# A quantized feed-forward stage whose instructions are put in a fixed order, five turns deep

## The chip, the cores and the metric

The kernel runs on one core of a Trainium2 chip. A core has five engines that follow their own instruction streams and meet at semaphores: TensorE (matmuls and transposes, written PE in profiles, its weight loads PEld), VectorE (DVE), ScalarE (ACT), GpSimd (POOL) and SyncE (SP, which issues the DMAs here). The metric is the device time of one execution in microseconds (us). Before the change the median of 8 runs is 2927.6 us, the lowest 2920.58 and the highest 2935.03.

## The reference, cut to what matters

The program computes a two-layer network on 64 x 64 tokens of 256 values. Layer 0 is attention and a feed-forward, layer 1 a recurrence with a state-space block and a mixture of experts. The change touches only the feed-forward of layer 0, `x = x + ffn(cond2(x, cond))`:

```python
ys = y * scale
d = rsqrt(einsum('bi,io->bo', ys * ys, weight * weight) + EPS)
out = einsum('bsi,io->bso', Efou * ys[:, None, :], weight) * d[:, None, :]
# bitlinear, twice: 256 -> 1024, then 1024 -> 256
x_norm = x * rsqrt(mean(square(x)) + EPS_NORM) * w
scale = 127.0 / clip(max(abs(x_norm)), 1e-5, None)
x_q = clip(round(x_norm * scale), -128, 127) / scale
h = x_q @ weight_quant(w1).T
h = act_scale * square(relu(h)) + act_bias      # between the two
```

Every token is thus multiplied by its sample's row `ys` and by a weight, scaled by `d`, normalised, rounded to whole numbers, multiplied by a ternary weight, squared behind a relu, normalised and rounded again, multiplied by a second ternary weight and added to x.

## The kernel before, in words

The residual x lies transposed in on-chip memory (`g.xT`: 128 partitions x 2 x 4096 tokens). `ffn0` (L560) walks over 16 pairs of token tiles; a pair is 2 x 128 tokens, `TP` = 256. The work on one pair `p` is cut into seven stages:

- `product` (L614): GpSimd multiplies the pair's x by `ys` into `xs` (L617). TensorE multiplies `xs` by `Wc` (L628) and spreads the rows of `d` with a selecting matmul (L632). ScalarE copies that spread out of PSUM (`dt`, L634), VectorE multiplies both into `gm` (L635), and ScalarE takes the sums of squares of `gm` (L581, which for a tile of 1024 columns is the "large" form).
- `quantize_in` (L638, through `quantized`, L584): first a refined inverse root of the mean of squares, on two numbers per partition. GpSimd forms the mean (L592), ScalarE takes the root (L593), VectorE the reciprocal (L594), and GpSimd a Newton step in five small operations (L595 to L599). Then VectorE multiplies the tile by the norm's weight (L600), takes the largest absolute value (L601), forms the scale (L603, L604), scales and rounds (L609), and writes whole numbers as bf16 (L611). GpSimd forms the scale back (L605, L606).
- `turn`: four transposes of that into PSUM (L645), copied by ScalarE to `qT` (L647).
- `up`: 2 x 2 matmul groups to 1024 columns (L655), a relu with a scale (L656) and a square (L658) on ScalarE, `act_scale` and `act_bias` on VectorE (L659), and the large sums of squares on ScalarE (L581).
- `quantize`: `quantized` again, on `h` (128 x 2048).
- `turn_back`: sixteen transposes (L670), copied by ScalarE to `q2T` in two halves (L671).
- `down`: sixteen matmuls (L678), the scale back on ScalarE (`o`, L680), four transposes (L682), the residual add on VectorE into xT (L684) and a DMA of x to HBM on SP's queue.

The loop writes them for a skew of seven: in turn `t`, pair `t` is in `product`, pair `t-1` in `quantize_in`, and so on, the latest stage first. That is only the order in which the operations are written. The framework's scheduler then orders each engine's stream by a priority that follows the written order and by its own estimate of when things are ready, places tiles in the pools' buffers, and adds the semaphores. A tile pool with `bufs=2` gives a name two buffers; PSUM has four buffers of the tag `ps` and four of the tag `acc`. What stands next to what on an engine is thus the scheduler's choice.

Behind the stage comes the recurrence of layer 1 (`rnn`), 64 steps that each need the one before. Its first matmuls (L723) over the second half of the samples need the last pair's residual add.

Of the kernel before, what the change touches and what calls it, by code (L numbers as in the profile page):

```python
# [13 lines left out]
F32 = mybir.dt.float32  # L14
BF16 = mybir.dt.bfloat16
I32 = mybir.dt.int32
AF = mybir.ActivationFunctionType
ALU = mybir.AluOpType
AX = mybir.AxisListType
PSUM = bass.MemoryType.PSUM  # L20

P = 128
B, L, D = 64, 64, 256
NT = B * L
CH = 512
NCH = NT // CH
KD = D // P
CB = CH // L
NTT = NT // P
EPS = 1e-8  # L30
MAGIC = 12582912.0
# [45 lines left out]
def bank(g, shape=(P, CH), dt=F32, tag="ps"):  # L77
    tag = g.tag or tag
    return g.psum.tile(list(shape), dt, tag=tag, name=tag)
# [477 lines left out]
    return chain(one, two, (squares, sums)), (lambda: rsqrt(nc, d2[:, 0, :], d, d2[:, 1, :]),)  # L557


def ffn0(g, w):  # L560


    nc, tc = g.nc, g.tc
    F = w.F
    NF = F // P
    T = 2
    TP = T * P
    NP = NT // TP
    BP = TP // L
    with (  # L570
        tc.tile_pool(name="f1", bufs=1) as p1,
        tc.tile_pool(name="f2", bufs=2) as p2,
        tc.tile_pool(name="f3", bufs=3) as p3,
    ):
        w1q, m1, w2q, m2, ys, d = w.w1q, w.m1, w.w2q, w.m2, w.ys, w.d

        def square_sums(x, n):
            ss = p2.tile([P, T], F32, name=f"ss{n}")
            for t in range(T):
                junk = p1.tile([P, n], BF16, name=f"junk{n}")  # L580
                nc.scalar.activation(junk, x[:, t, :], AF.Square, accum_out=ss[:, t : t + 1])  # L581
            return ss

        def quantized(x, ss, wn, mean, n):  # L584

            st = p3.tile([P, 7, T], F32, name=f"st{n}")  # L590
            v, rs, t, most, am, sc, back = (st[:, i, :] for i in range(7))
            nc.gpsimd.tensor_scalar(v, ss, 1.0 / n, EPS, ALU.mult, ALU.add)  # L592
            nc.scalar.activation(rs, v, AF.Sqrt)  # L593
            nc.vector.reciprocal(rs, rs)  # L594
            nc.gpsimd.tensor_mul(t, rs, rs)  # L595
            nc.gpsimd.tensor_mul(t, t, v)
            nc.gpsimd.tensor_scalar(t, t, -0.5, 1.5, ALU.mult, ALU.add)
            nc.gpsimd.tensor_mul(rs, rs, t)
            nc.gpsimd.tensor_scalar(most, rs, 127.0 / 1e-5, None, ALU.mult)  # L599
            nc.vector.tensor_tensor(x, x, wn.unsqueeze(1).to_broadcast([P, T, n]), ALU.mult)  # L600
            nc.vector.tensor_reduce(am, x, AX.X, ALU.max, apply_absolute_value=True)  # L601

            nc.vector.reciprocal(sc, am)  # L603
            nc.vector.scalar_tensor_tensor(sc, sc, 127.0, most, ALU.mult, ALU.min)  # L604
            nc.gpsimd.tensor_mul(back, am, rs)  # L605
            nc.gpsimd.tensor_scalar(back, back, 1e-5, mean, ALU.max, ALU.mult)  # L606
            q = p2.tile([P, T, n], BF16, name=f"q{n}")
            for i in range(T):
                nc.vector.tensor_scalar(x[:, i, :], x[:, i, :], sc[:, i : i + 1], MAGIC, ALU.mult, ALU.add)  # L609

            nc.vector.tensor_scalar(q, x, MAGIC, 127.0, ALU.subtract, ALU.min)  # L611
            return q, back

        def product(p, v):  # L614
            tok = ts(p, TP)
            xs = p2.tile([P, KD, BP, L], F32, name="xs")
            nc.gpsimd.tensor_tensor(  # L617
                xs,
                g.xT[:, :, tok].rearrange("p k (b l) -> p k b l", l=L),
                ys[:, :, ts(p, BP)].unsqueeze(3).to_broadcast([P, KD, BP, L]),  # L620
                ALU.mult,
            )
            xs2 = xs.rearrange("p k b l -> p k (b l)")
            gm = p2.tile([P, T, D], F32, name="gm")
            for t in range(T):
                ps = bank(g, (P, 2, D))
                for k in range(KD):
                    nc.tensor.matmul(ps[:, 0, :], xs2[:, k, ts(t, P)], w.Wc[:, k, :], start=(k == 0), stop=(k == KD - 1))  # L628

                for j in range(2):  # L630
                    b = p * BP + 2 * t + j
                    nc.tensor.matmul(ps[ts(j, L), 1, :], g.ident[:B, b : b + 1].to_broadcast([B, L]), d, start=True, stop=True)  # L632
                dt = p2.tile([P, D], F32, name="dt")
                nc.scalar.copy(dt, ps[:, 1, :])  # L634
                nc.vector.tensor_mul(gm[:, t, :], ps[:, 0, :], dt)  # L635
            v.gm, v.ss1 = gm, square_sums(gm, D)

        def quantize_in(p, v):  # L638
            v.q1, v.back1 = quantized(v.gm, v.ss1, w.n1, m1, D)

        def turn(p, v):
            pt = bank(g, (P, KD, TP), BF16)
            for t in range(T):
                for k in range(KD):
                    nc.tensor.transpose(pt[:, k, ts(t, P)], v.q1[:, t, ts(k, P)], g.identb)  # L645
            v.qT = p2.tile([P, KD, TP], BF16, name="qT")
            nc.scalar.copy(v.qT, pt)  # L647

        def up(p, v):
            v.h = p3.tile([P, T, F], F32, name="h")  # L650
            for t in range(T):
                for f in range(F // CH):
                    ps = bank(g)
                    for k in range(KD):
                        nc.tensor.matmul(ps, v.qT[:, k, ts(t, P)], w1q[:, k, ts(f, CH)], start=(k == 0), stop=(k == KD - 1))  # L655
                    nc.scalar.activation(v.h[:, t, ts(f, CH)], ps, AF.Relu, scale=v.back1[:, t : t + 1])  # L656
                h = v.h[:, t, :]
                nc.scalar.activation(h, h, AF.Square)  # L658
                nc.vector.tensor_scalar(h, h, w.act[:, 0:1], w.act[:, 1:2], ALU.mult, ALU.add)  # L659
            v.ss = square_sums(v.h, F)  # L660

        def quantize(p, v):
            v.q2, v.back2 = quantized(v.h, v.ss, w.n2, m2, F)

        def turn_back(p, v):
            v.q2T = p2.tile([P, T, NF, P], BF16, name="q2T")
            for t in range(T):
                pt = bank(g, (P, NF, P), BF16, tag="acc")
                for f in range(NF):
                    nc.tensor.transpose(pt[:, f, :], v.q2[:, t, ts(f, P)], g.identb)  # L670
                nc.scalar.copy(v.q2T[:, t], pt)  # L671

        def down(p, v):
            po = bank(g, (P, KD, TP), tag="acc")
            for t in range(T):
                ps = bank(g, tag="acc")
                for f in range(NF):
                    nc.tensor.matmul(ps[:, :D], v.q2T[:, t, f, :], w2q[:, f, :], start=(f == 0), stop=(f == NF - 1))  # L678
                o = p2.tile([P, D], F32, name="o")
                nc.scalar.activation(o, ps[:, :D], AF.Copy, scale=v.back2[:, t : t + 1])  # L680
                for k in range(KD):
                    nc.tensor.transpose(po[:, k, ts(t, P)], o[:, ts(k, P)], g.ident)  # L682
            x = g.xT[:, :, ts(p, TP)]
            nc.vector.tensor_add(x, x, po)  # L684
            nc.sync.dma_start(g.x[:, :, ts(p, TP)], x)

        stages = (product, quantize_in, turn, up, quantize, turn_back, down)
        pairs = [SimpleNamespace() for _ in range(NP)]
        for turn_ in range(NP + len(stages) - 1):
            for i in reversed(range(len(stages))):  # L690
                p = turn_ - i
                if 0 <= p < NP:
                    stages[i](p, pairs[p])

# [1272 lines left out]
def tile_adaln_attn_ffn_d2(ctx: ExitStack, tc: tile.TileContext, a: dict, out: bass.AP):  # L1969
# [29 lines left out]
    close_attn()  # L1999

    ffn0(g, w_ffn0)
    close_ffn0()

# [101 lines left out]
```

## Time and profile before

| what | value |
|---|---|
| median of 8 runs | 2927.6 us |
| profiled execution | 2927.91 us, of which span 2925.9 us |
| granted TensorE clock, whole span | 0.912 |
| the stage: first `xs` to the end of the last residual add | 383.4 to 637.6 us |
| busy in 383 to 638 us (255 us): PE, PEld, DVE | 185.05, 108.21, 201.78 us |
| the same: ACT, POOL | 187.30, 127.15 us |
| granted TensorE clock in that stretch | 0.83 |

The profile is of one execution. A row of the timeline gives the start, the length, the engine, the line, the operation, the tile written and the tiles read, the shape, how many are merged, and in brackets the idle time before it with what ended it. A row of the waits gives the one who waited, the one waited for, the total, how often, and the longest. Lengths on an engine overlap a little, since it begins the next step before the last is written; where a step's share of the engine is wanted, starts are compared with starts. The granted clock is the share of full speed at which TensorE was let run.

### The profile page before, as it was taken

To read this page: it belongs to the slowest core of one execution; us is meant where nothing else is said; L and a number is where in the kernel's file an instruction comes from. 1 tells how busy PE (TensorE), PEld (TensorE's weight loads), DVE (VectorE), ACT (ScalarE), POOL (GpSimd) and SP (SyncE) were. 2 spreads that over 40 slices of the span, in tenths; PEclk is the share of its full clock that TensorE was granted. 3 is DMA by queue.
4 is the path that set the end of the run, shared out by engine and by line. 5 is a ranking of instruction groups with operands and counts; after the bars stand their busy time and mean duration, and the time that the engine had idled before them with its cause. 6 is when DMAs were issued, how large, how long until landed. Compare 5 with 4: busy or idle time off the path is not lost.

```text
span 2925.9 us, 34770 instructions
## 1 busy us (share of the span) xinstructions
PE 2418.3 (83%) x12148; PEld 1707.8 (58%) x12148; DVE 1756.9 (60%) x2955; ACT 1412.6 (48%) x2406; POOL 1306.5 (45%) x1117
## 2 busy tenths in 40 slices
PE   4889977779566888888778888788885989999995
PEld 4533434458244555555455555466763768888885
DVE  0567658850399979798979888873352523232322
ACT  1566557764555666666565757443331212222220
POOL 0022345430368676768576868654536251111110
PEclk9979988798677989899889999899997999999997
DMA  9999600020122212121112121315685746655555
GB/s 235 369 358 337 212 25 19 19 66 1 44 73 77 71 59 76 64 74 66 58 62 98 62 90 69 112 35 179 199 279 193 275 172 245 221 184 204 204 186 178
DMA packets 183076, 406.06 MB, mean 139 GB/s; under 512 B 25312, under 2 KB 89056, under 8 KB 177520
## 3 DMA queue, kind: packets, MB, share of 16 engines
q1 hardware_dynamic: 169456, 366.80, 37.1%
q0 software_dynamic: 13440, 36.98, 3.3%
q8 instruction: 98, 1.61, 0.2%
q14 instruction: 82, 0.67, 0.1%
HBM read 280.76 MB, written 144.98 MB: 146 GB/s over the span
## 4 chain that ended last, share of the span: by engine, by line
PE 43%; DVE 19%; ACT 9%; issue 8%; POOL 5%; DMA 2%; another core or an unknown queue 1%; DVEq 0%; SPq 0%; ACTq 0%; POOLq 0%
DVE hb L1009 11%; PE ps L1603 11%; PE acc L1501 8%; DVE hb L1011 3%; PE yp L1025 2%; PE mq L1739 2%; PE mp L906 2%; PE ps L1570 2%; PE mq L1755 2%; POOL hb L970 2%; DVE xc L851 1%; PE ps L745 1%; PE ps L628 1%; PE acc L745 1%
## 5 line engine op out<-in xcount | busy, mean ns | idle before, releaser
L970 POOL TENSOR_TENSOR hb<-dx,Bn 128x1024 f32<-128x1024 f32 x256 | 600.9, 2357 | 259.2 <-PE yp L1025 253.5
L1009 DVE TENSOR_TENSOR_SCAN hb<-dA,hb 128x512 f32<-128x512 f32 x512 | 603.1, 1209 | 34.7 <-ACT dA L977 32.3
L977 ACT ACTIVATE dA<-delta,A 128x504 f32<-128x504 f32 x512 | 344.4, 683 | 306.3 <-DVE hb L1009 297.5
L1025 PEld LDWEIGHTS yp<-ident,hb 128*128 128x128 f32 x2048 | 267.0, 151 | 180.0 <-issue 141.9
L1011 DVE TENSOR_TENSOR hb<-hb,cb 128x1024 f32<-128x1024 f32 x256 | 312.2, 1220 | 79.3 <-PE cb L922 62.0
L1603 PE MATMUL ps<-gxT,w 128*128 128x256 f32 (+1 forms) x1600 | 323.7, 361 | 0.8 <-DVE gxT L1478 0.8
L1603 PEld LDWEIGHTS ps<-gxT,w 128*128 128x128 f32 x1600 | 276.5, 190 | 46.1 <-issue 12.5
L1025 PE MATMUL yp<-ident,hb 128*128 128x128 f32 x2048 | 301.4, 291 | 0.0
L1739 PE MATMUL mq<-x,moe_s 128*128 128x256 f32 x896 | 253.8, 416 | 50.8 <-ACT up L1746 27.0
L1277 POOL DMA_INDIRECT ffn_y<-gy,to x72 | 69.2, 961 | 446.6 <-ACT gy L1503 434.7
L1739 PEld LDWEIGHTS mq<-x,moe_s 128*128 128x128 f32 x896 | 171.2, 207 | 117.0 <-ACT up L1746 35.9
L1607 DVE TENSOR_TENSOR gh<-gs,ps 128x256 f32<-128x256 f32 (+1 forms) x200 | 78.7, 394 | 219.3 <-ACT gs L1606 217.3
L922 PE MATMUL cb<-parts,pick 80*128 80x512 bf16 x256 | 104.8, 409 | 111.2 <-DVE hb L1011 94.0
L1501 PE MATMUL acc<-w,gh 128*128 128x256 f32 (+1 forms) x864 | 191.6, 392 | 2.0 <-issue 2.0
L1503 ACT ACTIVATE gy<-acc,wt 128x256 f32<-128x256 f32 x152 | 67.1, 472 | 254.7 <-PE acc L1501 225.1
L1606 ACT ACTIVATE gs<-ps 128x256 f32<-128x256 f32 (+1 forms) x200 | 72.3, 362 | 241.0 <-PE ps L1603 224.9
L1501 PEld LDWEIGHTS acc<-w,gh 128*128 128x128 f32 (+1 forms) x864 | 148.3, 192 | 34.5 <-issue 16.7
L426 POOL TENSOR_TENSOR E<-E,z 128x1024 f32<-128x1024 f32 x32 | 61.6, 1924 | 202.8 <-DVE z L425 123.5
L1501 PE MATMUL acc<-w,rh 128*128 128x256 f32 x320 | 86.3, 411 | 50.6 <-ACT rh L1572 44.8
L1277 POOL DMA_INDIRECT moe_y<-gy,to x80 | 77.2, 965 | 112.0 <-ACT gy L1503 91.4
L444 PE MATMUL out<-oT,M 128*128 128x512 f32 x256 | 120.1, 614 | 1.5 <-ACT oT L437 1.5
L1755 PE MATMUL mq<-moe_s,sh 128*128 128x256 f32 x448 | 115.4, 396 | 6.2 <-ACT up L1746 6.2
(462 smaller groups left out, 4469.4 us busy)
## 6 DMA issues: line engine op xcount, KB each, us to landing
w<-ffn_w SPq DMA_DIRECT2D x40, 2176.0 KB
Bn<-B SPq DMA_DIRECT2D x128, 512.0 KB
moe_x<-fill SPq DMA_DIRECT2D x130, 260.0 KB
ffn_x<-fill SPq DMA_DIRECT2D x129, 260.0 KB
w<-moe_w SPq DMA_DIRECT2D x48, 512.0 KB
ffn_w<-in_ffn_W_dram SPq DMA_DIRECT2D x16, 640.0 KB
gx<-moe_x SPq DMA_DIRECT2D x32, 260.0 KB
gx<-ffn_x SPq DMA_DIRECT2D x32, 260.0 KB
```

Source lines behind the costliest of these rows:

```text
L444: nc.tensor.matmul(ps, M[:, o, ts(k, P)], v.o[:, o], start=(o == 0), stop=(o == H // 2 - 1))
L922: nc.tensor.matmul(t, pick[:, n : n + 1].to_broadcast([rows, P]), v.parts, start=True, stop=True)
L970: nc.gpsimd.tensor_mul(hb, vs[c].dx[p], Bn[:, n % NB, :].unsqueeze(1).to_broadcast([P, PI, CH]))
L977: nc.scalar.activation(decays[s][i][:, :, 1:], seq(vs[c].delta[p][:, i, :])[:, :, 1:], AF.Exp, scale=w.A[:, p * PI + i, n : n + 1],)
L1009: ins = nc.vector.tensor_tensor_scan(h, dA[i].rearrange("p b l -> p (b l)"), h, 0.0, ALU.mult, ALU.add)
L1011: ins = nc.vector.tensor_tensor(hb, hb, cb.unsqueeze(1).to_broadcast([P, PI, CH]), ALU.mult)
L1025: nc.tensor.matmul(yp[i][:, t, :], hb[:, i, ts(t, P)], g.ident, start=(n == 0 and t == 0), stop=(n == S - 1 and t == CH // P - 1), is_tran ...
L1277: i = self.g.nc.gpsimd.indirect_dma_start(out=self.y, out_offset=bass.IndirectOffsetOnAxis(ap=to, axis=0), in_=y, in_offset=None)
L1501: nc.tensor.matmul(po[s], h, w, start=(i == 0), stop=(i == n - 1))
L1603: nc.tensor.matmul(ps[:, j, :], v.w12[:, k, ts(j * (full + 1) + i, P)], v.xT[:, k, :], start=(k == 0), stop=(k == KD - 1))
L1739: nc.tensor.matmul(ps[:, i % 2, :], w[:, k, ts(i, P)], xu[:, k, :], start=(k == 0), stop=(k == KD - 1))
L1755: nc.tensor.matmul(ps[:, t, :], h[:, i, ts(t, P)], self.s2[:, i, :], start=(i == 0), stop=(i == NS - 1))
```

## The change

A small class, `InOrder`, wraps an engine: every operation that is asked through it gets a mark with the engine's name, and the scheduler keeps marked operations of one name in the order in which they were written. All operations of `ffn0` on TensorE, VectorE, ScalarE and GpSimd go through such wrappers, so their order on each engine is that of the text. Work of other stages is not marked.

The stages are cut into smaller pieces and written out once per turn in a fixed order, `turn_at(n)`. In turn `n`, pair `n` is in `product`, `n-1` is quantized and turned, `n-2` is in `up`, `n-3` is quantized on its 1024 columns and turned back, and `n-4` goes `down`; so the depth is five turns in place of seven. The first operation of a pair, GpSimd's product `xs`, becomes a piece of its own (`spread`) and is written one turn early: behind VectorE's large product and the refined root, ahead of the large maximum. The two halves of `up` are parted by `lie_down` and `product`. No operation, shape or buffer count changes. Since each operation is now issued from inside the wrapper, a profile shows nearly all of the stage under the wrapper's one line.

```diff
+class InOrder:
+    def __getattr__(self, op):
+        def ask(*args, **kwargs):
+            ins = getattr(self.engine, op)(*args, **kwargs)
+            self.tc.stamp_issue_order_token(ins.ins, self.name)
+            return ins
+        return ask
...
-        def quantized(x, ss, wn, mean, n):
+        def quantized(x, st, wn, mean, n, *between):
...
+            ve.tensor_tensor(x, x, wn.unsqueeze(1).to_broadcast([P, T, n]), ALU.mult)
+            for other in between:
+                other()
+            ve.tensor_reduce(am, x, AX.X, ALU.max, apply_absolute_value=True)
...
-        stages = (product, quantize_in, turn, up, quantize, turn_back, down)
-        for turn_ in range(NP + len(stages) - 1):
-            for i in reversed(range(len(stages))):
-                p = turn_ - i
-                if 0 <= p < NP:
-                    stages[i](p, pairs[p])
+            def quantize(p, v):
+                rest = (lambda: better(v.st2)), (lambda: at(spread, n + 1))
+                v.q2, v.back2 = quantized(v.h, v.st2, w.n2, m2, F, *rest)
+            def quantize_in(p, v):
+                better(v.st1)
+                v.q1, v.back1 = quantized(v.gm, v.st1, w.n1, m1, D)
...
+            at(quantize_in, n - 1)
+            at(down, n - 4)
+            at(root_big, n - 3)
+            if 0 <= n - 3 < NP:
+                at(quantize, n - 3)
+            else:
+                at(spread, n + 1)
+            at(up, n - 2, 0)
+            at(lie_down, n - 4)
+            at(product, n)
+            at(up, n - 2, 1)
+            at(turn, n - 1)
+            at(turned, n - 1)
+            at(modulated, n)
+            at(root_small, n)
+            at(turn_back, n - 3)
+            at(add, n - 4)
+            at(scaled, n - 2)
+            at(sums, n - 2)
+        at(spread, 0)
+        for n in range(NP + 4):
+            turn_at(n)
```

The pieces: `roots` is the mean (L592) and the root, `better` the reciprocal and the Newton step, `modulated` the copies of `dt`, the product `gm` and its sums of squares, `turned` the copy to `qT`, `scaled` the step of L659, `sums` the large sums of squares, `lie_down` the four transposes of `o`, `add` the residual add with its DMA.

## The prediction

> **What bounds the kernel now.** I read first the tile view of the residual xT, which dates the stage; then the busy time by stretch with the granted clock; then the waits inside the stage; then the timeline of each engine over two pairs, for durations.
>
> The tile view of xT, then the busy times (columns: stretch, its length, then PE, PEld, DVE, ACT, POOL, then the granted TensorE clock, DMA):
>
> ```profile
> L684 DVE TENSOR_TENSOR xT<-xT,acc x16: 672/684/689, 438.7 to 636.9; 128x512 f32<-128x512 f32 x16
> ```
>
> ```profile
> 470.00:588.00 118.00, 89.51 (x510) 52.11 (x509) 98.63 (x166) 89.58 (x184) 60.05 (x134) 0.80 0.06 19
> 498.05:515.12 17.07, 12.19 (x90) 7.26 (x88) 15.34 (x25) 15.93 (x33) 9.94 (x18) 1.00 0.09 31
> 515.12:528.77 13.65, 11.33 (x40) 6.26 (x41) 9.88 (x19) 7.09 (x16) 5.47 (x17) 0.50 0.01 2
> ```
>
> The stage runs from 383.4 (first product) to 637.6 (the last residual add, 636.92 + 0.69); the recurrence behind it needs that add. No engine is full in the middle: DVE 98.63 of 118. The two lower rows show one period of 30.7 us, two pairs: TensorE has its full clock for 17.07 us, then half for 13.65 us, and then the other engines starve (ACT 7.09 of 13.65). A pair costs about 15.2 us.
>
> ```profile
> PE acc L678 <- ACT q2T L671: 34.1, 15, 4.0
> ...
> DVE st L604 <- POOL st L599: 19.3, 8, 3.6
> ```
>
> So before is bound by waits between engines: TensorE for the evicted transposes q2T, VectorE for the small steps on GpSimd.
>
> ```profile
> 500.35 2.15 POOL L595 TENSOR_TENSOR st<-st 128x2 f32<-128x2 f32 x1 [2.02 <-DVE st L594]
> ```
>
> ```profile
> 621.11 2.31 POOL L592 TENSOR_SCALAR st<-ss 128x2 f32<-128x2 f32 x1 [2.19 <-ACT junk L581]
> ```
>
> These two-element steps last 0.19 us at other places. Here they started beside VectorE's large product L600 (500.18 and 621.08, 2.27 us) and ended with it. Beside the maximum L601 they take 0.19.
>
> ```profile
> 513.20 1.25 ACT L656 ACTIVATE h<-ps,st 128x512 f32<-128x512 f32 x2
> 514.47 1.06 ACT L658 ACTIVATE h<-h 128x1024 f32<-128x1024 f32 x1
> 515.43 0.40 ACT L581 ACTIVATE junk<-gm 128x256 bf16<-128x256 f32 x1
> ...
> 515.83 1.90 ACT L671 COPY q2T<-acc 128x1024 bf16<-128x1024 bf16 x2
> 517.63 0.21 ACT L593 ACTIVATE st<-st 128x2 f32<-128x2 f32 x1
> ```
>
> ```profile
> 533.74 1.08 PE L628 MATMUL ps<-Wc,xs 128*128 128x256 f32 x4
> ...
> 536.98 0.94 PE L678 MATMUL acc<-w2q,q2T 128*128 128x256 bf16 x7
> 537.75 1.03 PE L655 MATMUL ps<-w1q,qT 128*128 128x512 bf16 x4
> 538.77 0.44 PE L682 MATMUL acc<-ident,o 128*128 128x128 f32 x2
> ```
>
> Read starts against starts: two relus 1.27, a square 0.96, two q2T copies 1.80; at full clock a whole product (533.74 to 536.98) 3.24, one down matmul 0.11, four up matmuls 1.02.
>
> ```profile
> 627.39 0.17 DVE L603 RECIPROCAL st<-st 128x2 f32<-128x2 f32 x1
> 627.66 0.16 DVE L604 SCALAR_TENSOR_TENSOR st<-st 128x2 f32<-128x2 f32 x1
> 627.86 1.42 DVE L609 TENSOR_SCALAR h<-h,st 128x1024 f32<-128x1024 f32 x2
> 629.31 1.23 DVE L611 TENSOR_SCALAR q<-h 128x2048 bf16<-128x2048 f32 x1
> ```
>
> VectorE steps that need the one just before start after its end; unrelated ones start about 0.08 us before it.
>
> **The change, part by part.** No matmul, activation, vector or GpSimd operation is added or removed, nor a DMA; only their places move. On every engine and on SP's queue the work outside the stage stands in the same order as before, but for the first recurrence matmuls, which differ by some places on TensorE. So the price is the shift of the last add.
>
> *Steady turn, the ring.* ScalarE's order is now o, o, root, relu, relu, square, relu, relu, square, qT, dt, dt, two small square sums, root, q2T, q2T, two large square sums; TensorE's is down, up, lie_down, product, up, turn, turn_back. So down waits for the q2T copies, and these stand behind everything that ScalarE owes to this turn's product; behind them wait the large sums and the next turn's o copies, and for these lie_down. The ring at full clock, from one q2T to the next: q2T copies 1.80; large sums 2 x 1.04 = 2.08 (539.70 to 540.74); two o copies 0.84; last lie_down pair 0.34; product 3.24; half an up 0.64; two relus 1.27; square 0.96; qT copy 0.47; dt copy 0.41; gm product on VectorE 0.45; small sums 0.9; first GpSimd step 0.5 (0.19, held beside the product L659 as such steps are at 518.26: 0.69); root 0.15. Sum 14.05; four places where a step waits for the one ahead on its own engine (0.11 to 0.2) make it 14.5.
>
> *The clock.* From the relus to the q2T copy TensorE has only turn and turn_back (1.1 us) in some 6 us. In the trace such a stretch (511.9 to 515.1, transposes alone) is followed by half clock, as the third row shows. Down and the first up then take 2 x 2.8 us. TensorE's leg up to lie_down (first q2T 1.05, down 1.76, up 1.02) is 3.8 at full clock, 5.6 with down alone at half, 6.6 with both, against ScalarE's 4.7 (1.80 + 2.08 + 0.84): the cost is 0, 0.9 or 1.9. I take 0.8, near the middle, as down and up are dense enough to end the half rate. Turn: 15.3. Ends: 14.5, and with the product at half clock too (5.92 in the chain of waits, 520.23 to 526.15, 2.7 more) 14.5 + 1.9 + 2.7 = 19.1.
>
> [...]
>
> *VectorE's share.* Its own work per pair, starts against starts, is 8.28 for h (2.19 + 2.20 + 1.32 + 1.13 + 1.44), 2.72 for gm, 0.60 for the add, 0.45 for six small steps: 12.05. The dependent chains now stand unmixed: five pairs in each of two, 0.11 to 0.15 more each, 1.2. The small chain waits some 0.5 for GpSimd, whose first step is held by the gm product. 13.7 in all, under the ring, so hidden. [...]
>
> *The moved GpSimd product* (1.04 us): it now runs inside the 2.2 us maximum, where GpSimd is not held. Five small steps at 0.28 and the product end at 2.7 after the maximum starts, 0.3 past it. Behind it in GpSimd's queue stand only the two scale steps for o, due a turn later. Hidden below the ring; uncovered it costs 0.3 x 16 = 5 us; a gain is excluded, since nobody waits for the product early.
>
> *Fill.* Turns 1 and 2 hold product, up and ScalarE's part alone, some 8 us each, turn 3 13.4, turn 4 15.3 to 16: from 388 for the first gm product (386.7 before) the first add ends near 436, against 439.4. Gain 3 (ends 0 and 6).
>
> *Eleven turns* (pairs 0 to 11): 11 x 15.3 = 168.3, to 604; before, 600.6.
>
> *Drain.* With no product left, another ring binds: q2T copies 1.80, large sums 2.3, GpSimd's first step 2.39 (the 621.11 row: VectorE starts the large product on the same signal, so this step is always held), root and reciprocal 0.32, maximum 2.30, 0.47, scaling 1.45, rounding 1.24, eight transposes 0.7 to 1.0: 13.1. Three of them, 39.3, then the last q2T copy 1.0, down 1.8 to 3.2, o and lie_down 1.0, add 0.7: from 604.9 to about 650. Before, those four pairs took 37.0 (600.6 to 637.6).
>
> Sum: the last add at 650 against 637.6, +12.5. The profiled execution took 2927.91 us (span 2925.9, 2.0 around it), 0.3 above the median 2927.6, so 2940.5.
>
> **The rivals.**
>
> 1. *The ring does not bind, VectorE does* (not slower). Place: the q2T copy; price 13.7 instead of 15.3. 436 + 11 x 13.7 + 46 = 633, so 2923. It decides if the ring falls under 13.7, 0.8 less than summed at full clock. For it: VectorE is the busiest engine (98.63 of 118). Against: ring and half clock are summed from rows.
> 2. *TensorE keeps its full clock.* 14.5 x 11 instead of 15.3 x 11 saves 9, the drain 3: 638, 2928.5, no change. Against: every transposes-only stretch in the trace ends in half clock.
> [...]
> 4. *The order isn't held* (no change, 2928): the built program stands in it, so I leave it under 0.01.
>
> **How the numbers follow.** Forecast 0.75, rival 1 0.09, rival 2 0.07, rival 3 0.09. About 0.2%, 5.9 us, is what a measurement of this kernel can tell from no change. The forecast's own range is 2932 to 2950 (turn 15.3 +- 0.5, fill and drain +- 3); I widen it to 2931 and 2954 towards rivals 2 and 3. Slower: all of rival 3 and nearly all of the forecast, 0.84. Same: rival 2, most of rival 1, a rest of the forecast, 0.13. Faster: the end of rival 1, 0.03.
>
> **What the changed profile would show.** All steps under one line (the wrapper's), so tiles tell them apart. Right: the last xT add near 650; adds some 15.3 apart, then 13 in the last three turns; TensorE waiting for q2T once a turn for 3 to 4 us; one half-clock stretch in every turn, 3 to 7 us long; the GpSimd step on the large sums at 2.3 us in every turn; the xs product inside the large maximum at 1.04. [...] A shift of work outside 383 to 650 would make the whole account wrong.

## The result, and the profile after

The changed kernel takes 2942.26 us (median of 19 runs, 2934.97 to 2951.5) against 2929.58 for the kernel before (56 runs, 2919.97 to 2939.44): ratio 1.0043, 95% interval 1.0034 to 1.0052. It is 12.7 us slower; 2940.5 was forecast. In its own line order everything of the stage stands under L568, the wrapper's call, and lines behind the stage are 81 higher.

The tile view of xT dates the stage (duration min/median/max in ns, then first and last start):

```profile
L568 DVE TENSOR_TENSOR xT<-xT,acc x16: 677/678/686, 432.6 to 649.4; 128x512 f32<-128x512 f32 x16
```

The last add ends at 650.1 (637.6 before). The sixteen ends, read from the same records, split the 12.5 us:

| part | before | after | difference |
|---|---|---|---|
| end of the first add | 439.4 | 433.3 | -6.1 |
| eleven steps to the twelfth add | 161.2 | 169.4 (15.40 each) | +8.2 |
| the last four steps | 37.0 | 47.4 (13.8, 13.5, 13.0, 7.1) | +10.4 |

Of the 6.1 us, 2.4 are not the change's. The stage's first product `xs` starts at 381.0 us in this profile and at 383.4 in the one before, behind code that is the same in both; runs 8 and 11 below, which keep the old stages, have their first product matmul at 382.46 and 380.27 for 384.50, so this start moves by itself. Counted from the first `xs`, the first add comes 3.7 us sooner and the stage is 14.9 us longer.

So the fuller pipe starts sooner, each turn of it is longer, and it empties more slowly. The recurrence's first tanh starts 12.5 us later (652.8 for 640.3). The two profiled spans differ by 17.2 us; the other 5 lie behind the recurrence (2193.0 us from its last tanh to the end, 2187.5 before), in code that the change does not touch, and the medians do not show them.

Busy times by stretch of the changed kernel (stretch, length, PE, PEld, DVE, ACT, POOL, granted TensorE clock, DMA):

```profile
470.00:588.00 118.00, 81.88 (x495) 49.77 (x493) 101.09 (x160) 89.90 (x177) 59.10 (x129) 0.85 0.05 17
481.40:484.80 3.40, 3.04 (x15) 2.17 (x16) 2.56 (x7) 3.37 (x7) 1.93 (x7) 0.50 0.03 8
484.80:495.00 10.20, 7.15 (x51) 4.19 (x49) 9.37 (x12) 7.63 (x17) 5.45 (x10) 1.00 0.01 2
495.00:501.90 6.90, 5.34 (x22) 3.33 (x23) 5.98 (x11) 5.05 (x9) 4.47 (x9) 0.51 0.11 38
501.90:512.10 10.20, 5.97 (x44) 3.45 (x42) 8.33 (x15) 7.56 (x16) 3.64 (x10) 1.00 0.07 22
```

The period is again two pairs, 30.7 us. Where before had one stretch of 13.65 us at half clock in it, this one has two, of 3.4 and 6.9: one in each turn. The mean clock is even higher than before (0.85 against 0.80), and the turn is still no shorter.

All these stretches are multiples of about 3.41 us (1, 3, 2 and 3 here, 5 and 4 before), and the period of both kernels is nine of them. Cut at that step, the slow stretch of 6.9 has two parts; the third line is a part of the slow stretch before:

```profile
495.00:498.45 3.45, 1.89 (x9) 1.34 (x10) 3.03 (x9) 3.05 (x5) 2.17 (x8) 0.51 0.22 76
498.45:501.90 3.45, 3.45 (x14) 1.99 (x13) 2.95 (x4) 2.00 (x5) 2.30 (x2) 0.50 0.00 0
521.94:525.35 3.41, 3.41 (x11) 1.76 (x12) 2.03 (x4) 1.42 (x3) 0.16 (x1) 0.50 0.01 2
```

Down starts 0.4 us into the stretch at 481.4 and 1.6 us into the one at 495.0, and the second time the clock stays low for one step more. Pairs of turns settle at 15.92 + 14.80 = 30.72 us, and runs 2, 4 and 5 below, each with other work in the turn, settle at the same two numbers. So the turn keeps step with the clock here; whether the clock holds it there was not tested.

What the turn consists of is told by the chain of work that ended last, here a turn and the beginning of the next (start, length, engine and tile):

```profile
526.32 0.91 ACT q2T L568
...
527.27 3.59 PE acc L568 x16
530.87 1.71 PE ps L568 x4
532.57 0.51 PE acc L568 x4
533.08 3.64 PE ps L568 x18
...
536.74 1.27 ACT h L568 x2
...
538.04 1.06 ACT h L568
539.09 0.47 ACT qT L568
539.57 0.28 ACT dt L568
...
539.87 0.44 DVE gm L568
...
540.87 0.52 ACT junk L568 x2
...
541.46 0.54 POOL st L568
...
542.03 0.20 ACT st L568
542.23 0.91 ACT q2T L568
...
543.19 3.40 PE acc L568 x16
546.58 0.86 PE ps L568 x4
```

Read it as a ring: the first q2T copy, down (3.59), half of up (1.71), lie_down (0.51), the product with the rest of up (3.64), then relu, square, qT, dt, gm, the small sums, GpSimd's step, the root, and q2T again, 15.9 us later. In this turn down and the first up ran at half clock; in the next one down alone was slow (3.40) and up quick (0.86), and that turn was 14.8. The two alternate. In the list of waits (us in total, times, longest) TensorE stands idle for q2T once a turn:

```profile
PE acc L568 <- ACT q2T L568: 38.1, 16, 3.5
```

And the timeline of the same turn shows the two neighbours on VectorE and GpSimd (start, length):

```profile
530.39 2.29 DVE L568 TENSOR_TENSOR h<-h,n 128x2048 f32<-128x2048 f32 x1 [0.46 <-ACT junk L568]
533.08 2.27 DVE L568 TENSOR_REDUCE st<-h 128x2 f32<-128x2048 f32 x1
...
530.44 2.29 POOL L568 TENSOR_SCALAR st<-ss 128x2 f32<-128x2 f32 x1 [1.15 <-ACT junk L568]
534.54 1.04 POOL L568 TENSOR_TENSOR xs<-xT,ys 128x512 f32<-128x512 f32 x1
```

GpSimd's two-element step on the large sums lasts as long as VectorE's large product beside it. Its moved product xs starts 1.46 us into the maximum, takes the same 1.04 us as elsewhere, and ends 0.2 after it; the maximum keeps its 2.27.

### The profile page after: what moved, and what is told of

It is laid out like the page before. It is cut to its first block, busy times and chain, and to the rows that moved or that the text cites. A ratio compares the mean times of both kernels' runs of the same rounds, so it can differ in the third digit from the quotient of the medians.

```text
span 2943.1 us, 34806 instructions
## 1 busy us (share of the span) xinstructions
PE 2420.7 (82%) x12148; PEld 1716.5 (58%) x12148; DVE 1766.2 (60%) x2955; ACT 1419.5 (48%) x2406; POOL 1301.2 (44%) x1117
## 4 chain that ended last, share of the span: by engine, by line
PE 43%; DVE 20%; ACT 8%; issue 8%; POOL 5%; DMA 2%; another core or an unknown queue 2%; DVEq 0%; SPq 0%; ACTq 0%; POOLq 0%
DVE hb L1090 12%; PE ps L1684 11%; PE acc L1582 8%; DVE hb L1092 3%; PE ps L568 2%; PE ps L1651 2%; PE acc L568 2%; POOL hb L1051 2%; PE yp L1106 2%; PE mp L987 2%; PE mq L1820 2%; PE mq L1836 1%; DVE xc L932 1%; PE ps L826 1%
## 5 line engine op out<-in xcount | busy, mean ns | idle before, releaser
L1820 PEld LDWEIGHTS mq<-x,moe_s 128*128 128x128 f32 x896 | 172.4, 208 | 118.1 <-ACT up L1827 35.6
```

The costliest lines, as they stand in the source:

```text
L1820: nc.tensor.matmul(ps[:, i % 2, :], w[:, k, ts(i, P)], xu[:, k, :], start=(k == 0), stop=(k == KD - 1))
```

## The experiments

All ratios are to runs of the kernel before on the same chip in the same sitting, since chips differ: in the sitting of the first four runs the kernel before took 2876.53 us, in that of the next four 2933.26, in the last 2937.69. The changed kernel, at 1.0043, is 12.6 us behind before in these terms. It was not run again in those sittings, so a comparison with its ratio leans on ratios being alike from chip to chip. Turn means the mean of the eleven steps from the first add to the twelfth, drain the four steps after that.

### 1. Six matmuls in TensorE's wait

```diff
             for t in range(T):
                 ps = bank(g, tag="acc")
+                for i in range(6 if t == 0 else 0):
+                    te.matmul(ps, w1q[:, 0, :P], w1q[:, 0, :CH], start=True, stop=True)
                 for f in range(NF):
```

> Added: six matmuls (128x512, on the weights w1q, into the bank that down is about to overwrite) ahead of down in TensorE's order, so that they lie in its wait for q2T (2.4 us a turn in the changed kernel). Theory (the ring goes q2T, down, first up, lie_down, product, second up, relus, square, qT, dt, gm, small sums, root, q2T, and down and the first up run at half clock): from the end of a q2T copy to the end of lie_down TensorE takes 5.9 us in a slow turn (527.22 to 533.08) and 4.7 in a quick one, while ScalarE's own leg there (second copy, large sums, two o copies, last transposes) would allow 4.3; with the clock kept the steps of 15.8 and 14.8 both become 14.3 to 14.5, eleven turns fall by 10, and the kernel by 10 to 12, to 2930 or a little under, level with the kernel before. Rival (the half clock is covered by ScalarE's leg or by VectorE): 0, 2942. Rival (six matmuls are too many for the wait): slower by up to 6 x 0.43 us a turn, 2980.

Ratio 1.0017 (1.0005 to 1.0029). The turn is 14.48, every step 14.4 to 14.5 with no alternation; the drain is 47.6, unchanged. Eleven turns give back 10.1 us, as expected; the ratio says 7.6, with intervals of some 3 us each. The granted clock in the same stretch, in this kernel:

```profile
470.00:588.00 118.00, 91.76 (x563) 52.74 (x560) 106.39 (x171) 95.93 (x189) 61.03 (x136) 0.91 0.06 19
```

TensorE does more work, its granted clock is 0.91 for the changed kernel's 0.85, and the kernel is faster: the half clock was on the ring, at 0.9 us a turn. What binds next is in the chain of the same kernel:

```profile
519.83 1.06 ACT junk L568 x2
520.91 1.16 ACT junk L568 x2
...
522.14 2.30 POOL st L568
...
524.70 2.36 DVE st L568 x2
...
527.54 1.43 DVE h L568 x2
...
530.14 0.43 DVE gm L568
```

Down and up are gone from it. The chain now runs through the large sums, the step of 2.3 us, the maximum, scaling and rounding, and then through gm and the small sums back to q2T. The changed kernel has all the links of this second ring too; it is 0.9 us shorter than the mean turn of the first.

### 2. GpSimd's product once in place of sixteen times

```diff
-            xs2 = v.xs.rearrange("p k b l -> p k (b l)")
+            xs2 = pairs[0].xs.rearrange("p k b l -> p k (b l)")
...
-                rest = (lambda: better(v.st2)), (lambda: at(spread, n + 1))
+                rest = (lambda: better(v.st2),)
```

> Left out: GpSimd's product xs is computed for the first pair alone and every pair multiplies by that tile; fifteen products of 1.04 us, all beside the large maximum, are gone. Theory (hidden): 2942, within 3 us. Rival (the product's 0.2 us past the end of the maximum, or its reading beside the maximum, holds VectorE): 0.2 to 1.0 us a turn, 3 to 15 us faster.

Ratio 1.0025 (1.0011 to 1.0039), turn 15.47, drain 47.4, last add 268.6 us after the stage's first product matmul, against 15.40, 47.4 and 268.0 in the changed kernel. The stage is not shorter without the product, so beside the maximum it costs nothing. The ratio alone would not have settled it: it lies 5 us under the changed kernel's, the two intervals only just overlap, and the trace shows no place for these 5 us in the stage.

### 3. GpSimd's product beside the scaling

```diff
-                rest = (lambda: better(v.st2)), (lambda: at(spread, n + 1))
+                rest = (lambda: better(v.st2),)
...
             at(quantize, n - 3)
+            at(spread, n + 1)
```

> Moved: GpSimd's product xs stands behind the two scale steps of the large quantizing, so that it meets VectorE's scaling and rounding passes in place of the maximum. Theory (the ring has slack there): the rounding may be late by up to 1.04 us, but its transposes end at 539.65 and the q2T copy starts at 542.23, so nothing is later: 2942 to 2945. Rival (the place beside the maximum is what makes it free): VectorE is held for 1.04 us a turn on the path, up to 16 us slower, 2958.

Ratio 1.0035 (1.0021 to 1.0048), turn 15.47; the last add comes 271.4 us after the first product matmul (268.0 in the changed kernel). The ratio is no higher than the changed kernel's; the trace has the stage 3.4 us longer, 3.3 of them ahead of the first add. That is the theory's 0 to 3, not the rival's 16. But the operations themselves changed. Tile views of this kernel from 470 to 588:

```profile
L568 DVE TENSOR_SCALAR h<-h,st x16: 752/1142/1534, 477.8 to 587.5; 128x1024 f32<-128x1024 f32 x16
...
L568 POOL TENSOR_TENSOR xs<-xT,ys x8: 1503/1506/1511, 478.0 to 587.0; 128x512 f32<-128x512 f32 x8
```

In the changed kernel xs takes 1042 ns and the scaling 751 ns each time. Here xs starts 0.14 us into the first of two scalings and takes 0.46 us more, where 0.61 of that scaling was left; the second scaling takes 0.78 more. Why the two lengthen beside each other is not shown. VectorE loses 0.8 us a turn, and the ring, which did not go through the scaling, hides it: a real gain of the place beside the maximum, worth nothing while TensorE's ring is the longer.

### 4. The step on the large sums on VectorE

```diff
-        def roots(ss, n):
+        def roots(ss, n, by=pe):
...
-            pe.tensor_scalar(v, ss, 1.0 / n, EPS, ALU.mult, ALU.add)
+            by.tensor_scalar(v, ss, 1.0 / n, EPS, ALU.mult, ALU.add)
...
-                v.st2 = roots(v.ss, F)
+                v.st2 = roots(v.ss, F, ve)
```

> Moved: the first step on the large sums (one step a pair, two elements) from GpSimd, where it lasts 2.3 us beside VectorE's large product, to VectorE ahead of that product (0.2 us). Theory A (the term of the drain as the prediction worded it: GpSimd's held step is a link of the ring of 13.1): three to four turns of the drain lose 2.1 us each, 6 to 8 us faster, 2935. Theory B (the reciprocal behind it stands on VectorE behind the large product, which overwrites h in place and so waits for the same sums; the held step only runs beside that product): at most 0.2 us a turn, 2941 to 2943. In the steady turns both expect nothing, since the ring there does not pass through this step.

Ratio 1.0033 (1.0021 to 1.0045), turn 15.46, drain 45.5 (13.5, 13.2, 12.8, 6.0). Each of the three ring turns of the drain lost 0.3 us, near theory B's 0.2 at most and far from A's 2.1; the last step lost 1.1, which neither foresaw. The step fell from 2.3 to 0.17 us and almost nothing came of it: GpSimd's held step was beside the path, not on it.

### 5. The norm's product into a tile of its own

```diff
-            ve.tensor_tensor(x, x, wn.unsqueeze(1).to_broadcast([P, T, n]), ALU.mult)
+            h, x = x, p1.tile([P, T, n], F32, name=f"xn{n}")
+            ve.tensor_tensor(x, h, wn.unsqueeze(1).to_broadcast([P, T, n]), ALU.mult)
```

> Changed: the product with the norm's weights is written to a tile of its own, not over its input, so VectorE's large product no longer waits until ScalarE has read h for the large sums. Theory (that wait is what the term of 2.3 in the drain was): in the drain the large product can run from 617.9, as the scaling ends, in place of 621.2; GpSimd's first step on the sums is then not held (0.2 in place of 2.3), the maximum starts some 2.0 us earlier in each of three turns, the drain falls from 47.4 to about 41, and the kernel by 6, to 2936 by the scale of the changed kernel's 2942 (ratio to before near 1.002). In the steady turn, whose ring does not pass there, nothing. Rival (the drain is bound by ScalarE and TensorE with the half clock): 0, ratio 1.004.

Ratio 1.0023 (1.0006 to 1.0039), turn 15.46, drain 42.3 (13.2, 12.0, 11.2, 5.8): 5.1 us off the drain, none off the turns. (The edit serves both norms, the small one on gm too.) The timeline of the changed kernel in the drain, and then of this one:

```profile
621.20 2.29 DVE L568 TENSOR_TENSOR h<-h,n 128x2048 f32<-128x2048 f32 x1 [3.27 <-ACT junk L568]
621.25 2.29 POOL L568 TENSOR_SCALAR st<-ss 128x2 f32<-128x2 f32 x1 [7.86 <-ACT junk L568]
```

```profile
616.10 2.29 DVE L568 TENSOR_TENSOR xn<-h,n 128x2048 f32<-128x2048 f32 x1
...
619.39 0.19 POOL L568 TENSOR_SCALAR st<-ss 128x2 f32<-128x2 f32 x1 [7.86 <-ACT junk L568]
...
620.54 2.27 DVE L568 TENSOR_REDUCE st<-xn 128x2 f32<-128x2048 f32 x1
```

In the first VectorE idles for 3.27 us until ScalarE has read h for its sums, since the product overwrites h; the step on GpSimd merely runs alongside. In the second the product is over when the sums end, the step takes 0.19 us, and the maximum starts 1.15 us after it began (2.64 in the changed kernel, 621.25 to 623.89). Runs 4 and 5 together name the cause of these 5.1 us: the reuse of h, not the held step. The drain was 10.4 us longer than before; the other 5.3 stay without a cause shown.

### 6. The same stages with the order free

```diff
             ins = getattr(self.engine, op)(*args, **kwargs)
-            self.tc.stamp_issue_order_token(ins.ins, self.name)
             return ins
```

> Undone: the set order. The stages, their split and the order in which they are asked for are those of the changed kernel, but no engine is held to it. Theory (the set order is the cost): in the changed kernel the transposes for q2T end at 539.65, while ScalarE, held behind dt, the small sums and the root, copies at 542.23, 2.6 us later; free, it copies when they are there, and a turn falls from 15.4 towards 14.0 to 14.8, eleven turns by 7 to 15: ratio to before 0.999 to 1.002. Rival (the stages five deep, with their dependences, set 15.4 a turn whatever the order): 1.004.

Ratio 0.999 (0.9975 to 1.0005), turn 14.23, drain 43.7, last add at 632.4. Without the set order the new stages are level with the kernel before. Holding the engines to this order costs 15 us, all of the loss and a little more; the five-deep staging itself costs nothing that can be measured.

### 7. The set order with the old stages

The edit wraps all four engines of the kernel before as the change does, and leaves its seven stages as they are.

```diff
+        te, ve, se, pe = (InOrder(tc, getattr(nc, n), n) for n in ("tensor", "vector", "scalar", "gpsimd"))
```

> The other half alone: the stages of the kernel before, seven deep, with every engine held to the order in which that kernel writes them. Theory (an order has to be written for being held: here ScalarE's large sums stand behind VectorE's scaling of the same turn, its qT behind the small quantizing, and dt behind qT, so that VectorE's 12 us of a pair and ScalarE's and TensorE's parts follow one another): 20 to 30 us a turn, 80 to 240 us slower, ratio 1.03 to 1.08. Rival (the scheduler keeps nearly the written order anyway): within 1% of before.

3142.0 us in a single execution, 1.071 times before. Its tile view:

```profile
L568 DVE TENSOR_TENSOR xT<-xT,acc x16: 680/689/690, 484.6 to 850.7; 128x512 f32<-128x512 f32 x16
```

The adds are 24.4 us apart on average. Of the change's two halves, the staging is what makes the set order bearable, and the set order is what makes the staging lose.

### 8. The kernel before with eight matmuls in the wait

```diff
                 ps = bank(g, tag="acc")
+                for i in range(8 if t == 0 else 0):
+                    nc.tensor.matmul(ps, w1q[:, 0, :P], w1q[:, 0, :CH], start=True, stop=True)
                 for f in range(NF):
```

> The kernel before with eight matmuls (128x512, on w1q, into the bank that down is about to overwrite) ahead of each pair's first down, in the wait for q2T (34.1 us in 15 waits). Theory (half clock costs the kernel before more than the changed one): its adds stand 13.0 and 17.4 apart in turn, the long ones with the half-clock stretches; if the clock holds, all come 13.0 to 13.4 apart, eleven turns fall from 161.2 to 143 to 148, the kernel by 13 to 18 us: ratio 0.994 to 0.996. Rival (the clock falls anyway, or the matmuls delay down by up to 8 x 0.22 us a pair): 1.000 to 1.010.

Ratio 0.9956 (0.9936 to 0.9976): 12.9 us faster than before. Turn 13.12 (14.66 before), drain 38.0. The granted clock from 470 to 588 was 0.80 in the kernel before:

```profile
470.00:588.00 118.00, 92.33 (x603) 56.94 (x615) 109.97 (x183) 100.56 (x203) 68.99 (x145) 0.94 0.06 21
```

VectorE's share rises from 98.63 to 109.97 of 118. The matmuls are worth 1.5 us a pair here and 0.9 in the changed kernel, so the half clock probably cost the kernel before more. But here the scheduler orders everything anew: in one of the two pairs from 497 to 530 us it puts the next product between the extra matmuls and down. Clock and order are thus not parted in this run, as they are in run 1, and the steps came 11.5 to 14.0 apart, not 13.0 to 13.4.

### 9. Both edits under the set order

The edits of runs 1 and 5 in the changed kernel.

> Both edits of the first and the fifth run in the changed kernel, its set order kept: six matmuls ahead of down, and the norm's product in a tile of its own. Theory (the clock costs the steady turns, the overwritten h the drain; they do not overlap): the first run's turn of 14.5 (10 us in eleven turns) and the fifth run's drain of 42.3 (5 us) together, 15 us off the changed kernel's 12.6 above before: ratio 0.998 to 1.000. Rival (in the drain the half clock takes back what the own tile gives): 1.001 to 1.002.

Ratio 0.9997 (0.9983 to 1.0011), turn 14.41, drain 43.8 (47.6 with the filler alone). The theory holds for the whole: the two edits take back all of the 12.6 us. The drain is still not as short as before (43.8 against 37.0); to make up for it, the turn is now 0.24 us under the 14.66 of the kernel before, and the first add comes 4 us sooner after the first product matmul. And the drain is 1.5 us longer than run 5's 42.3, all of it in the last step, 7.3 for 5.8, in which six of the matmuls stand. The theory does not hold for a shorter turn: with the wait on h gone as well, the turn only went from 14.48 to 14.41. The chain of this kernel says why:

```profile
521.14 1.01 ACT q2T L568
522.15 1.06 ACT junk L568 x2
...
523.23 1.15 ACT junk L568 x2
524.38 0.37 ACT o L568
...
524.80 0.80 PE acc L568 x4
525.60 3.63 PE ps L568 x16
...
529.26 1.28 ACT h L568 x2
```

This is the ring that the prediction summed at 14.5 for full clock, link by link: both q2T copies, the large sums, o, lie_down, product, up, relu and on. With the extra matmuls (granted clock 0.94 from 470 to 588 in this kernel, 0.91 in run 1) there are two rings of 14.4 to 14.5, this one and that of run 1.

### 10. Both edits with the order free

The edits of runs 1, 5 and 6.

> The same two edits with the order free as in the sixth run. Theory: the sixth run's 0.999 less up to 0.7 us a turn for the 78 us at half clock that it still had (the first run went from 95 to 65 and gained 10 us) and 3 to 5 us in the drain: ratio 0.993 to 0.997, so faster than both kernels. Rival (free, the scheduler already works around the half clock, and the six matmuls land where TensorE is wanted): 0.998 to 1.003.

Ratio 0.9985 (0.997 to 1.0). The theory's range is missed and the rival's holds. The turn is 14.36, no shorter than with the order free alone (14.23). The chain:

```profile
537.99 3.64 PE ps L568 x10
541.63 2.29 PE acc L568 x22
543.92 1.20 PE ps L568 x4
545.12 1.75 PE acc L568 x16
546.87 0.43 PE ps L568 x2
547.31 0.57 PE acc L568 x4
```

TensorE's work now follows on itself for 10 us, so TensorE is wanted where the extra matmuls stand. Why the order chosen has it all in one piece was not tried.

### 11. The kernel before, with ten matmuls and a tile of its own

The edits of runs 8 (with ten) and 5 in the kernel before.

> The kernel before with ten matmuls ahead of each pair's first down and the norm's product in a tile of its own. Theory: the eighth run's 0.9956 less 0 to 5 us, since its adds in the drain were 9.3, 9.5 and 6.9 apart, not 13 as in the changed kernel, so that little of the drain waits on the overwritten h: 0.993 to 0.996. Rival (ten matmuls of 0.22 to 0.43 us outlast the wait for q2T): 0.997 to 1.003.

Ratio 0.993 (0.9916 to 0.9943): 2918.26 against 2937.69 us. Turn 13.30, drain 35.6, last add at 615.4 (637.6 before). It is faster than both kernels, and 5 us (by the last add, counted from the first product matmul: 235.1 for 240.3) faster than run 8, the upper end of the theory. Of these the drain gave 2.4, as the theory had it; the turns took 2.0 back, and the first add came 4.8 earlier, which the theory did not foresee.

## Why the prediction was right

- **Place and sum.** The price was to be the shift of the last add. Predicted 650, measured 650.1. That it is so close is luck: the stage took 14.9 us longer, where 12.5 was forecast, and in this profile it began 2.4 us earlier. The medians' 12.7, with an interval from 10.0 to 15.2, fits both.
- **The ring and its links.** The order of links was right. At full clock 14.5 was summed; run 9, whose chain is this ring, gives 14.41 at a granted clock of 0.94 (470 to 588). Of the two legs that the working put side by side from the first q2T copy up to lie_down, TensorE's at half clock was the longer, as it said, but each time less long: 6.25 with down and up slow (526.32 to 532.57; 6.6 predicted), 5.21 with down alone (542.23 to 547.44; 5.6).
- **The clock term.** 0.8 a turn was taken between 0, 0.9 and 1.9; run 1 measures 15.40 less 14.48, 0.9, as the mean of a slow turn (15.9, 1.4 more) and a quick one (14.8, 0.3 more); with the second ring out of the way, runs 5 and 9 give 15.46 less 14.41, 1.05. The size is in part luck. Down and up were taken to be dense enough to end the half rate. No run shows that dense work ends it: down ran at half clock in both turns shown (3.59 and 3.40 us, 1.76 expected at full clock), and up in the first (1.71; 0.86 in the second). By the prediction's own prices for what came, 1.9 and 0.9, the mean would have been 1.4. Each price was some 0.5 us too high. Rival 3, half clock through the product (19.1 a turn at the upper end), did not come: the product takes 3.64 in both turns shown.
- **The return of the clock.** In the changed kernel, after the stretch of 3.40 us with TensorE busy for 3.04, the full clock came back; the stretch of 6.90 was busy for 1.89 in its first half and for all of its second, and then it came back. In the kernel before, though, a part of 3.41 us that was busy throughout (521.94 to 525.35) was followed by another at half clock (0.50 from 525.35 to 528.77): the busy time that a profile shows does not alone say when the clock returns.
- **VectorE.** Its 13.7 was to be under the ring, and is. What was missed is the second ring of run 1: the drain's 13.1 was said to bind only with no product left, but in steady turns it closes through gm and the small sums at 14.48. Nothing followed from that for the time, since the first ring was longer.
- **GpSimd's product.** Costed at 0; run 2 shows 0, run 3 shows what the place spares.
- **Fill.** Gain 3 predicted, with ends 0 and 6; 6.1 measured, of which 2.4 are the earlier start of the stage, so 3.7.
- **Drain.** About 45 us predicted, 47.4 measured. The three ring turns were put at 13.1 each and took 13.8, 13.5 and 13.0. The tail came to 7.1 us: its down was put at 1.8 to 3.2 us, and the chain shows 4.02 for eighteen TensorE instructions of that tile at its place. The sum also let the drain begin at 604.9, where its eleven turns end at 604.3; the twelfth add ended at 602.7.
- **The reason for the drain's 2.39.** The size was right and the reason was only half right. The prediction counted GpSimd's held step as the link and noted beside it that the product starts on the same signal. Run 4 shows the step to be no link; run 5 shows that the product's wait on h is.
- **The signs.** Adds 15.3 apart (alternately 14.8 and 15.9), then 13: seen. One half-clock stretch a turn of 3 to 7 us: seen. GpSimd's step at 2.3 us and xs at 1.04 inside the maximum: seen. TensorE's wait for q2T at 3 to 4 us was too long: it is 2.4 on average, 3.5 at most.
- **Two readings that do not hold.** "Every transposes-only stretch in the trace ends in half clock" stood against rival 2. In the kernel before, TensorE has transposes alone from 500.26 us and then nothing until 502.87, and the clock stays full (1.00 from 498.05 to 515.12); it fell within the stretch from 511.86 to 516.88, nearly twice as long. And a pair did not cost 15.2 us before: the eleven steps come to 14.66 each. No term of the sum used that number.
- **Rival 2** (full clock, 2928.5, no change) was tested in the turns only. Run 1 raised the clock there (0.83 to 0.92 between the first and the twelfth add) and was at 1.0017. In its drain the clock was 0.79, for 0.78 in the changed kernel, and the drain as long as ever, so the 3 us that the rival had for the drain were not tested.

## What to carry to other kernels

Before holding engines to a written order, sum the ring that the order closes over all engines at once, with each engine's steps as the order puts them, and look for a second ring just below it: taking away the first then gains only the difference. When TensorE idles for some microseconds in each turn (2.4 on average in the changed kernel), count what the turn pays at half clock (0.9 us in run 1); matmuls on operands that lie ready in that very wait can be worth more than a new schedule (12.9 us off the kernel before in run 8), as long as the engine is not wanted there. An operation that writes over its input waits for every reader of that input (VectorE stood idle for 3.27 us ahead of its large product), and a small step that lengthens beside it (2.29 us, 0.19 in run 5) will look like the culprit.

## What the runs showed of the hardware

Work added to TensorE shortened the kernel: with eight matmuls of 128x512 a pair the granted clock was 0.94 for 0.80 in the stretch from 470 to 588 and the kernel before 12.9 us faster, its order changed as well (run 8); with six and the order held it was 0.91 for 0.85, and the turn 0.9 us shorter (run 1). GpSimd's 128x512 product costs VectorE nothing beside the maximum (1042 ns, maximum 2266). Beside the scaling both took longer (run 3): the product 1506 ns, and the second scaling up to 1534 in place of 751, while the first, which had run for 0.14 us when the product began, kept its 752. What lengthens them no run here shows.

The stretches of full and half clock shown here last multiples of about 3.41 us in both kernels (3.4, 6.9 and 10.2; 13.65 and 17.07).
